# A four-layer network on one core: the first element's expert combination and first scan preparation spread over attention units, and the sorting's pool opened earlier

## The chip, the cores and the metric

The kernel runs on one core of a Trainium2 chip, in float32. The time is device microseconds (us) from start to end of one execution. A core has five engines that run beside each other, each with its own queue of instructions worked off in order: TensorE (PE, matrix products; its weight loads are listed as PEld), VectorE (DVE), ScalarE (ACT), GpSimd (POOL) and SyncE (SP, which issues most transfers). Engines wait for each other by semaphores. A waiting instruction holds everything behind it on its own engine. Matrix products go to a small accumulation memory (PSUM) of eight banks, which POOL does not read; all else lies in the on-chip memory SBUF, of 128 partitions.

## The reference

Four batch elements of 1024 tokens and 128 channels go through four layers. Each layer is a mixer and a feed-forward, each with a residual and a layernorm behind it:

```python
x = _layernorm(x + _L0_attn_ref(x, ...), axis=-1)   # two minGRU layers
x = _layernorm(x + _L0_ffn_ref(x, ...), axis=-1)    # routing to 64 slots
x = _layernorm(x + _L1_attn_ref(x, ...), axis=-1)   # attention of some queries
x = _layernorm(x + _L1_ffn_ref(x, ...), axis=-1)    # gated feed-forward
x = _layernorm(x + _L2_attn_ref(x, ...), axis=-1)   # 16-head linear attention
x = _layernorm(x + _L2_ffn_ref(x, ...), axis=-1)    # 8 experts, top 2 of them
x = _layernorm(x + _L3_attn_ref(x, ...), axis=-1)   # state-space scan
x = _layernorm(x + _L3_ffn_ref(x, ...), axis=-1)    # 8 experts, top-p of 0.8
```

The change touches the third layer's experts and the fourth layer's scan, whose cores are:

```python
# L2_ffn: two experts a token, weighted
y_sel = jnp.take_along_axis(y, indices[..., None], axis=2)
return (y_sel * weights[..., None]).sum(axis=2)
# L3_attn: x is RMS-normed; xc a causal convolution of x @ in_w.T over 4 tokens
xs = jax.nn.silu(xc.transpose(0, 2, 1))
delta = jax.nn.softplus(xs @ wd1.T @ wd2.T + wd2_b)
Bm = xs @ wb.T
Cm = xs @ wc.T
h = jnp.exp(d_l[:, :, None] * A) * h + (d_l * x_l)[:, :, None] * b_l[:, None, :]
y_l = jnp.einsum('ben,bn->be', h, c_l)
```

The scan has 256 channels and 16 states, so 16 x 256 recurrences over the tokens of each element.

## The kernel before, in words

**Attention of the third layer** (`l2_attn`, from L965). The work is 128 units: four elements, four quarters of 256 tokens each, eight pairs of heads. In iteration t of its loop the stages of neighbouring units are overlapped: `l2_project` of unit t+2 (PE product `pqk`; then the ACT relu of L1078 into `r_q` and `r_k`, and POOL's products `qt`, L1086), `l2_keys` and `l2_scores` of t+1 (`kN`, L1101; `pa_m`; DVE's mask `a`, L1144), `l2_before`, `l2_within` and `l2_out` of t (`po`, L1153; division on DVE). Every eight units `l2_values` makes the next quarter's values (`pv`, cast by DVE into `cv`), and every four `l2_project_out` transposes and projects the outputs (`pt`, `coT`, `pr`). The PE order of this part is the order in the program (a manual schedule). On the other engines, and in all that follows, a scheduler with a timeline model decides the order. `self.beat` is the latest unit's relu.

**Sorting** (`l2_dispatch`). After an element's attention its tokens are routed: softmax and ranks, positions by prefix sums, and 16 scatters on POOL (L1410, 128 rows of 512 bytes each) that put token rows into `xrows`, sorted by expert. For the first three elements each scatter has a dependency on the beat of its time, which spreads them; the last element's 16 are left in `self.m2["rest"]`, and the loop `l3` issues one per scan step. The dispatch's small tiles lie in the pool `md`, opened inside the attention's scope.

**Experts of the third layer** (`l2_ffn`, L1429). A generator works off 23 tiles of 128 sorted rows per element, advanced once per attention unit by `early(moe)`, and later per scan step. Per tile: two weight loads on SP (`wx`, L1485), row loads `xg` (L1469), transposes, the hidden products (into the attention's banks `pa_m`, later `ph`), ACT's sigmoid (L1517), the output products, store of results `ys` to `yrows` (L1539). It looks eight tiles ahead and waits there until the next element's rows are put. When an element's last tile is out, `l2_combine` (L1546) runs: 16 gathers on POOL (L1556) in two groups of 8 into the buffer `yg`, ACT copies scaled by the expert's weight (L1573, L1580), DVE additions of 128x512 (L1583, L1585), and the layernorm's parts (L163; square root on ACT at L177, normalisation at L187 and L191).

**Preparation of the scan** (`l3_prepare`, L1744). Once the first element is combined, the first of eight half-elements (element, half of 512 tokens) is prepared beside the last attention units, one generator step per unit: RMS norm, transposes `pt`, projection `pxe`, convolution of 3+1 terms on DVE, tanh, products `pdb` and `pd`, softplus by Exp and Ln on ACT (L1828, L1833), and DVE sums into `ud` and `dl`. `l3_early` tells where its tiles lie: in finished elements' transposed inputs `xT`, and in PSUM.

**Scan and fourth layer** (`l3`). For each half there are 16 steps, one per state (`l3_scan`, L1846): SP loads `bn` and `cn` (L1871, one row each spread over all partitions), POOL's product `db` (L1876, 128x1024), ACT's exponential `da` (L1880), two DVE scans (L1881), POOL's product `hc` (L1892), and PE's sum into `pys`. Beside the steps the loop advances the previous half's finish, the next half's preparation, the rest of the scatters, one expert tile (two in the first half) and the top-p experts of finished halves (`l3_experts`: weights `wh`, products `ph` and `py`, L2007, L2032). `l3` advances `moe` until an element is combined before it prepares that element's first half.

**Pools** (`program`, from L2194). Pools are opened and closed like a stack on either side of the memory: `keep`, `first`, `mt`, then `w2` (the attention's weights) on the right; `md` is opened inside `with w2`, and both are given back after the attention. `l3_pools` then opens the scan's pools over the room that has come free, so a scan tile waits for the last user of what lay there.

Of the kernel before, what the change touches and what calls it, by code (L numbers as in the profile page):

```python
# [12 lines left out]
F32 = mybir.dt.float32  # L13
# [3 lines left out]
ALU = mybir.AluOpType  # L17
# [3 lines left out]
P = 128  # L21
# [50 lines left out]
class Net:  # L72
# [874 lines left out]
    def l2_attn(self, load, dispatch, moe, first):  # L947
# [7 lines left out]
        with ExitStack() as ctx:  # L955
# [35 lines left out]
            for t in range(-2, n + 4):  # L991
                if t == 0:
                    load()
                if 0 <= t + 1 < n:
                    u = units[t + 1]
                    if u["hp"] == 0:
                        i = (t + 1) // NP2
                        if i + 1 < len(quarters):
                            nxt = quarters[i + 1]
                            self.l2_tiles(nxt, quarters[i])  # L1000
                            side.append(self.l2_values(nxt))
                    self.l2_keys(u)
                if 0 <= t + 2 < n:
                    self.l2_project(units[t + 2])
                if 0 <= t + 1 < n:
                    self.l2_scores(units[t + 1])
                if 0 <= t < n:
                    self.l2_before(units[t])
                    self.l2_within(units[t])
                if 0 <= t + 1 < n:  # L1010
                    self.l2_sums(units[t + 1])
                if "put" in self.m2["st"][0] if t > 0 else False:
                    early(moe)
                    if "done" in self.m2["st"][0]:
# [510 lines left out]
    def l2_expert_out(self, u, units, i, wp):  # L1525
# [12 lines left out]
        if j % 4 == n - 1:  # L1538
# [4 lines left out]
                in_=ys[:, 0:n, :],  # L1543
            )

    def l2_combine(self, st, wp):  # L1546

        nc, b = self.nc, st["b"]
        yg = {}

        def gather(h, c):
# [70 lines left out]
    def l3(self, moe, fp):  # L1622
# [98 lines left out]
    def l3_early(self, pool):  # L1721
# [5 lines left out]
        def at(name, shape):  # L1727
            if name in ("xnT", "tail", "xs3"):
                return pool.tile(shape, F32, name=name)
            if name in ("dl", "ud"):  # L1730
                return self.xT[1 if name == "dl" else 2].rearrange("p (e t) -> p e t", e=2)
            if name == "sq3":
# [3 lines left out]
            if name == "xc":  # L1736
                k[0] += 1
                return half(0, k[0] % 2)
            return half(0, name == "sp_w")[:, None, :]

        u = dict(b=0, h=0, at=at, ff=self.bank("pj"))
        self.c3["first"] = u
# [2 lines left out]
    def l3_prepare(self, u):  # L1745
# [2 lines left out]
        at, ff, dp = u.get("at", self.l3_at), u.get("ff", self.bank("ff")), c3["dp"]  # L1748
        wdb = c3["we"][:, :, 0:ND]

        sq = at("sq3", [P, 4, D])
        ms = self.sm.tile([P, 4], F32, name="ms3")
        for k in range(4):
            nc.scalar.activation(
                sq[:, k, :], self.xN[b][:, 4 * h + k, :], AF.Square, accum_out=ms[:, k : k + 1]
            )
        yield
        nc.scalar.activation(ms, ms, AF.Sqrt, bias=self.epsc, scale=1.0 / D)
        nc.vector.reciprocal(ms, ms)
        for k in range(4):  # L1760
            nc.scalar.activation(
                sq[:, k, :], self.xN[b][:, 4 * h + k, :], AF.Copy, scale=ms[:, k : k + 1]
            )
        yield
        pt = ff([P, 4, P], "pt")
        for k in range(4):
            self.tr(pt[:, k, :], sq[:, k, :])
# [2 lines left out]
            xnT, pt.rearrange("p a b -> p (a b)"), AF.Copy, scale=self.col("norm_w")  # L1770
        )
        yield

        K1 = KCONV - 1
        tail = at("tail", [P, 2, K1]) if h == 0 else u["prev"]["tail"]
# [2 lines left out]
        for ec in range(2):  # L1778
            p = ff([P, 512], "pxe")
            self.mm(p, c3["wskip"][:, 1, ec * P : (ec + 1) * P], xnT)  # L1780
            xc = at("xc", [P, 512])
# [4 lines left out]
            nc.vector.tensor_scalar(xc[:, o:], p[:, o:], w[K1], bias, ALU.mult, ALU.add)  # L1786
            if h:
                nc.vector.scalar_tensor_tensor(
                    xc[:, 0:K1], p[:, 0:K1], w[K1], tail[:, ec, :], ALU.mult, ALU.add
                )  # L1790
            for d in range(1, KCONV):
                nc.vector.scalar_tensor_tensor(
                    xc[:, d:], p[:, 0 : 512 - d], w[K1 - d], xc[:, d:], ALU.mult, ALU.add
                )
            if h == 0:
                nc.vector.tensor_scalar(
# [6 lines left out]
                    )  # L1803
            yield

            nc.scalar.activation(p, xc, AF.Tanh)
            nc.vector.scalar_tensor_tensor(xs[:, ec, :], p, 1.0, xc, ALU.add, ALU.mult)
# [9 lines left out]
        yield  # L1817

        dl, ud = at("dl", [P, 2, 512]), at("ud", [P, 2, 512])
        for g in ((0,), (1,)) if "at" in u else ((0, 1),):  # L1820
# [14 lines left out]
            for k, ec in enumerate(g):  # L1835
# [6 lines left out]
            if g[-1] == 0:  # L1842
                yield
        u.update(xnT=xnT, xs=xs, dl=dl, ud=ud, rows=rows)

    def l3_scan(self, u):  # L1846
# [351 lines left out]
def program(tc, io):  # L2198
    with ExitStack() as ctx:
# [9 lines left out]
        with ExitStack() as ff:  # L2209
# [37 lines left out]
```

## Time and profile before

| what | value |
|---|---|
| median of 3 runs | 2261.67 us (2253.73 to 2262.74) |
| the profiled execution | 2265.2 us, span 2263.4 us |
| mean granted PE clock | 0.934 |
| instructions | 46328 |
| attention units 105 to 109 begin, end | 1134.5, 1185.8 |
| last attention unit's projection begins | 1293.6 |
| first scan product `db` on POOL | 1363.5 |
| second half's first step | 1452.3 |
| first product of the top-p experts | 1525.1 |
| last scan product `hc` ends | 2126.8 |

The page's parts: totals per engine; the span in 40 slices; transfers; the chain of work that ended last; groups of instructions by source line with operands (`out<-in`, number, busy us, mean ns, idle time before them and its releaser). A line of the trace names engine, source line, operation and tile. Line numbers are those of the kernel shown. Sources are often helpers' lines, as L140 for every product and L177 for every square root of a layernorm, so the tile's name tells which one it is.

### The profile page before, as it was taken

The page shows a single profiled execution, that of the slowest core. Times are in us where ns is not written, and L with a number is a line of the kernel's source. Part 1 is how long each engine was busy: PE and PEld are TensorE (multiplying, and loading weights), DVE is VectorE, ACT ScalarE, POOL GpSimd, SP SyncE. Part 2 cuts the span into 40 slices and gives each one's busy share as a digit, 9 for nine tenths or more (in the row PEclk, how much of TensorE's full clock was granted, in tenths as well). Part 3 has the DMA queues.
Part 4 walks back from the last instruction along what each step waited for, and adds up shares of the span by engine and source line. Part 5 has one row for each costly group of instructions (what it writes and reads, how often), then busy time and mean ns, then how long its engine had stood idle before and what let it go on. Part 6 is the DMA issues. An engine that isn't in the chain of part 4 may idle for free.

```text
span 2263.4 us, 46328 instructions
## 1 busy us (share of the span) xinstructions
PE 1988.1 (88%) x17791; PEld 1392.3 (62%) x17791; DVE 1361.8 (60%) x3705; ACT 1184.6 (52%) x2578; POOL 1025.0 (45%) x813
## 2 busy tenths in 40 slices
PE   6778889899999999999979866688898999999998
PEld 3565555544577777787768654356565656565666
DVE  7767644433455654754555555696877688686522
ACT  6532434322344444454555556476768787676443
POOL 5100411000123244234143339989788889789400
PEclk9778979889999999999999987799999999999999
DMA  3010110050000000031222066466776676676421
GB/s 107 0 38 10 31 38 1 23 172 0 2 3 2 14 27 22 25 91 41 78 79 81 17 193 193 127 193 191 205 209 172 185 186 190 181 203 170 113 61 52
DMA packets 138605, 211.04 MB, mean 93 GB/s; under 512 B 18645, under 2 KB 75982, under 8 KB 137999
## 3 DMA queue, kind: packets, MB, share of 16 engines
q1 hardware_dynamic: 126238, 173.81, 25.4%
q0 software_dynamic: 12144, 34.26, 7.3%
q8 instruction: 140, 2.29, 0.4%
q14 instruction: 83, 0.67, 0.1%
HBM read 160.22 MB, written 23.16 MB: 81 GB/s over the span
## 4 chain that ended last, share of the span: by engine, by line
PE 44%; DVE 13%; ACT 10%; issue 3%; DMA 2%; POOL 1%; SPq 0%; DVEq 0%; ACTq 0%; POOLq 0%
PE py L140 8%; PE ph L140 7%; PE po L1153 5%; DVE db L1881 5%; PE pa_m L140 5%; PE pqk L140 5%; PE kp_mo L140 3%; PE pr L1223 2%; PE pys L140 2%; PE pv L140 2%; PE pt L144 1%; ACT da L1880 1%; ACT hh L2007 1%; PE kp_mo L144 1%; ACT xN L187 1%
## 5 line engine op out<-in xcount | busy, mean ns | idle before, releaser
L1086 POOL TENSOR_TENSOR qt<-r_q,sb_c_turn 128x256 f32<-128x256 f32 (+1 forms) x256 | 164.7, 664 | 451.0 <-ACT r_q L1078 447.1
L1892 POOL TENSOR_TENSOR hc<-db,cn 128x1024 f32<-128x1024 f32 x128 | 319.0, 2529 | 67.4 <-PE pys L140 26.8
L140 PEld LDWEIGHTS py<-wh,hh 128*128 128x128 f32 x2048 | 257.0, 196 | 79.8 <-issue 47.8
L1876 POOL TENSOR_TENSOR db<-ud,bn 128x1024 f32<-128x1024 f32 x112 | 293.1, 2679 | 7.6 <-ACT dl L1841 5.1
L140 PE MATMUL ph<-xT,wh 128*128 128x512 f32 x512 | 252.9, 611 | 24.0 <-ACT hh L2007 6.7
L140 PE MATMUL py<-wh,hh 128*128 128x128 f32 x2048 | 263.8, 280 | 10.8 <-ACT hh L2007 4.2
L2007 ACT ACTIVATE hh<-ph,sb_cols 128x512 f32<-128x512 f32 x256 | 170.3, 681 | 118.3 <-PE ph L140 92.1
L1144 DVE TENSOR_TENSOR a<-pa_m,sb_c_near 128x256 f32<-128x256 f32 x256 | 96.7, 419 | 201.4 <-PE pa_m L140 201.4
L1101 ACT ACTIVATE kN<-kp_mo,sb_c_trig 128x128 f32<-128x128 f32 x448 | 130.2, 372 | 130.6 <-PE kp_mo L144 122.4
L1880 ACT ACTIVATE da<-dl,aneg 128x512 f32<-128x512 f32 x224 | 153.6, 689 | 74.4 <-DVE db L1881 73.7
L140 PE MATMUL pys<-hc,sb_c_ident 128*128 128x512 f32 x324 | 160.6, 625 | 21.3 <-POOL hc L1892 17.9
L1881 DVE TENSOR_TENSOR_SCAN db<-da,carry,db 128x512 f32<-128x512 f32 x128 | 156.9, 1265 | 21.5 <-POOL db L1876 11.2
L1881 DVE TENSOR_TENSOR_SCAN db<-da,db 128x512 f32<-128x512 f32 x128 | 149.4, 1206 | 11.5 <-ACT da L1880 6.4
L140 PEld LDWEIGHTS ph<-xT,wh 128*128 128x128 f32 x512 | 88.0, 194 | 104.3 <-issue 49.0
L2032 DVE SCALAR_TENSOR_TENSOR h_acc<-py,gt,h_acc 128x128 f32<-128x128 f32 x252 | 70.8, 343 | 123.7 <-PE py L140 123.7
L140 PE MATMUL pqk<-xT,wE 128*128 128x256 f32 x512 | 136.4, 389 | 8.2 <-ACT coT L1220 4.2
L140 PEld LDWEIGHTS pys<-hc,sb_c_ident 128*128 128x128 f32 x324 | 61.1, 201 | 83.8 <-issue 57.7
L140 PEld LDWEIGHTS pqk<-xT,wE 128*128 128x128 f32 x512 | 88.5, 193 | 21.9 <-DVE cv L1063 8.1
L1220 ACT COPY coT<-pt 128x512 f32<-128x512 f32 x64 | 37.5, 587 | 116.8 <-PE pt L144 116.8
L140 PE MATMUL po<-ht,wD 128*128 128x512 f32 x192 | 92.9, 594 | 0.0
L1153 PE MATMUL po<-cv,a 128*64 128x65 f32 x2048 | 88.3, 228 | 0.0
L1556 POOL DMA_INDIRECT yg<-yrows,di x64 | 61.3, 957 | 57.5 <-DVE ch L1388 36.7
(463 smaller groups left out, 4255.2 us busy)
## 6 DMA issues: line engine op xcount, KB each, us to landing
wx<-in_wF SPq DMA_DIRECT2D x92, 384.0 KB, 3.4
bn<-rows SPq DMA_DIRECT2D x128, 256.0 KB, 4.7
cn<-rows SPq DMA_DIRECT2D x128, 256.0 KB, 4.2
wh<-in_wH SPq DMA_DIRECT2D x64, 512.0 KB, 3.8
hc<-hc POOLq DMA_DIRECT2D x47, 512.0 KB, 7.0
xrows<-zero SPq DMA_DIRECT2D x4, 1472.0 KB, 12.0
xg<-xrows SPq DMA_DIRECT2D x20, 256.0 KB, 3.6
yrows<-ys SPq DMA_DIRECT2D x20, 256.0 KB, 3.4
```

What stands on the lines that cost most here:

```text
L140: return self.nc.tensor.matmul(out=out, lhsT=lhsT, rhs=rhs, start=start, stop=stop)
L1086: nc.gpsimd.tensor_mul(u["qt"][:, m, a:], u["q"][:, a:], c2["turn"][:, m, o + a : o + 2 * P])
L1101: self.nc.scalar.activation(u["kN"][:, c, m, :], pk[:, c, :], AF.Copy, scale=trig[:, k, m : m + 1])
L1144: nc.vector.tensor_mul(u["a"][:, i, :, :], pa[i], self.c2["near"][:, None, :].to_broadcast([P, 2, P]),)
L1153: self.nc.tensor.matmul(out=u["po"][self.HALF[j], i, c, :], lhsT=lhsT, rhs=rhs, start=key not in u["begun"], stop=True, skip_group_check=True,
L1556: nc.gpsimd.indirect_dma_start(out=yg[h][:, k, c, :], out_offset=None, in_=st["out"][:, :], in_offset=bass.IndirectOffsetOnAxis(ap=st["des ...
L1876: nc.gpsimd.tensor_mul(db, ud, bc[0])
L1880: nc.scalar.activation(da, dl[:, ec, :], AF.Exp, scale=aneg[:, j : j + 1])
L1881: nc.vector.tensor_tensor_scan(db[:, ec, :], da, db[:, ec, :], carry[:, ec, n : n + 1] if h else 0.0, ALU.mult, ALU.add,)
L1892: nc.gpsimd.tensor_mul(hc, db, bc[1])
L2007: nc.scalar.activation(ht, ph, AF.Relu, bias=self.col("h_b1", i=e * NK + k))
L2032: nc.vector.scalar_tensor_tensor(acc[:, c, :], py[:, c, :], gt[:, c, e : e + 1], acc[:, c, :], ALU.mult, ALU.add,)
```

## The change

1. `l2_attn` advances the first preparation by a second step per unit.
2. `l2_ffn` is split: the tiles of elements 0 to 2, and behind their last combination those of element 3.
3. The first element's combination becomes a generator of its own, `l2_combine_first`. Its gathers, DVE multiply-adds (16 of 128x128 in place of 16 ACT copies and 4 DVE additions), one square root for all eight chunks, and four ACT and four DVE normalisations have a dependency on the beat of their unit. `yg0` (8 KB per partition) lies in `md`.
4. `l3` advances `rest`, the last element's scatters, only from the second half on.
5. The first preparation gets more steps and dependencies on the beat. The projection is copied from PSUM to SBUF by ACT, temporary tiles move into `md`, both channel halves share one Ln over 128x1024, and `dl` is summed in place instead of by a last ACT copy.
6. `md` is opened before the pool of the attention's weights.

```diff
@@ l2_attn
                     if next(g, self) is self:
                         side.remove(g)
+                if begin is not None:
+                    next(begin, None)
@@ l2_ffn
+        yield from self.l2_tiles_of(0, B - 1, wp)
+        yield from self.l2_tiles_of(B - 1, B, wp)
+
+    def l2_tiles_of(self, b0, b1, wp):
...
-            for st in self.m2["st"]
+            for st in self.m2["st"][b0:b1]
@@
+    def pace(self, i):
+
+        self.tc.add_manual_dep(i.ins, self.beat.name, SYNC, reason="spread out")
+        return i
+
+    def l2_combine_first(self, st):
...
+        def add(c):
+            for k in (1, 0):
+                self.pace(
+                    nc.vector.scalar_tensor_tensor(
+                        x[:, c, :], yg[:, k, c, :], st["wts"][k][:, c : c + 1], x[:, c, :],
+                        ALU.mult, ALU.add,
+                    )
+                )
+            v = self.sm.tile([P, 4, 6], F32, name="ln_st")
+            nc.vector.bn_stats(v[:, 0, :], x[:, c, :])
+            nc.vector.bn_aggr(mv[:, c, :], v[:, 0, :])
+
+        for c in range(NC + 3):
+            for k in range(2 if c < NC else 0):
+                self.pace(
+                    nc.gpsimd.indirect_dma_start(
...
+            if c >= 3:
+                add(c - 3)
+            yield
+        yield
+        self.pace(nc.scalar.activation(rs, mv[:, :, 1], AF.Sqrt, bias=self.epsc))
+        yield
+        yield
+        self.pace(nc.vector.reciprocal(rs, rs))
+        nc.vector.scalar_tensor_tensor(nm, mv[:, :, 0], -1.0, rs, ALU.mult, ALU.mult)
+        yield
+        yield
+        for c in range(0, NC, 2):
+            self.pace(
+                nc.scalar.activation(
+                    x[:, c, :], x[:, c, :], AF.Identity, bias=nm[:, c : c + 1], scale=rs[:, c : c + 1]
+                )
+            )
+            self.pace(
+                nc.vector.tensor_scalar(
+                    x[:, c + 1, :], x[:, c + 1, :], mv[:, c + 1, 0:1], rs[:, c + 1 : c + 2],
+                    ALU.subtract, ALU.mult,
+                )
+            )
+            yield
+        st["done"] = True
@@ l3
-                        next(moe)
+                        next(moe, None)
...
-                for k in range(1):
+                if i:
                     next(self.m2["rest"], None)
@@ l3_early
+            if name in ("sp_u", "sp_w", "tmp"):
+                return self.m2["md"].tile(shape, F32, name=f"e_{name}")
@@ l3_prepare
+            if early:
+                t = at("tmp", [P, 512])
+                nc.scalar.copy(t, p)
+                p = t
+                yield
...
+        if early:
+            yield
+            us, v = at("sp_u", [P, 2, 512]), at("sp_w", [P, 2, 512])
+            t = at("tmp", [P, 2, 512])
...
+            pace(nc.scalar.activation(v, v, AF.Ln))
+            for ec in range(2):
+                yield
+                d = dl[:, ec, :]
+                pace(nc.vector.tensor_sub(t[:, ec, :], us[:, ec, :], t[:, ec, :]))
+                pace(nc.vector.tensor_add(d, d, t[:, ec, :]))
+                pace(nc.vector.tensor_add(d, v[:, ec, :], d))
+                pace(nc.vector.tensor_mul(ud[:, ec, :], xs[:, ec, :], d))
@@ program
             w2 = ExitStack()
+            md = w2.enter_context(tc.tile_pool(name="moed", bufs=1, side="right"))
             n.l2_attn_load(w2.enter_context(tc.tile_pool(name="w2", bufs=1, side="right")))
...
         with w2:
-            md = w2.enter_context(tc.tile_pool(name="moed", bufs=1, side="right"))
             n.l2_attn(load, n.l2_dispatch, moe, first)
```

More of the change, by code (lines that the diff above doesn't have):

```diff
@@ L1544, in l2_expert_out @@
             )
+    def pace(self, i):
+        self.tc.add_manual_dep(i.ins, self.beat.name, SYNC, reason="spread out")
+        return i
+    def l2_combine_first(self, st):
+        nc, b, md = self.nc, st["b"], self.m2["md"]
+        yg = md.tile([P, 2, NC, D], F32, name="yg0")
+        mv = md.tile([P, NC, 2], F32, name="mv0")
+        rs = md.tile([P, NC], F32, name="rs0")
+        nm = md.tile([P, NC], F32, name="nm0")
+        x = self.xN[b]
+        def add(c):
[13 more added lines that the diff above has]
+                    nc.gpsimd.indirect_dma_start(
+                        out=yg[:, k, c, :],
+                        out_offset=None,
+                        in_=st["out"][:, :],
+                        in_offset=bass.IndirectOffsetOnAxis(
+                            ap=st["dest"][k][:, c : c + 1], axis=0
+                        ),
+                    )
[21 more added lines that the diff above has]
+                    ALU.subtract, ALU.mult,
+                )
+            )
+            yield
+        st["done"] = True
@@ L1546, in l2_combine @@
     def l2_combine(self, st, wp):
         nc, b = self.nc, st["b"]
+        if b == 0:
+            yield from self.l2_combine_first(st)
+            return
         yg = {}
@@ L1738, in at @@
                 return half(0, k[0] % 2)
-            return half(0, name == "sp_w")[:, None, :]
         u = dict(b=0, h=0, at=at, ff=self.bank("pj"))
@@ L1749, in l3_prepare @@
         wdb = c3["we"][:, :, 0:ND]
+        early = "at" in u
+        pace = self.pace if early else (lambda i: i)
         sq = at("sq3", [P, 4, D])
@@ L1753, in l3_prepare @@
         for k in range(4):
-            nc.scalar.activation(
-                sq[:, k, :], self.xN[b][:, 4 * h + k, :], AF.Square, accum_out=ms[:, k : k + 1]
+            pace(
+                nc.scalar.activation(
+                    sq[:, k, :], self.xN[b][:, 4 * h + k, :], AF.Square, accum_out=ms[:, k : k + 1]
+                )
+            )
+            if early and k == 1:
+                yield
+        yield
+        pace(nc.scalar.activation(ms, ms, AF.Sqrt, bias=self.epsc, scale=1.0 / D))
+        if early:
+            yield
+        pace(nc.vector.reciprocal(ms, ms))
+        for k in range(4):
+            if early and k % 2 == 0:
+                yield
+            pace(
+                nc.scalar.activation(
+                    sq[:, k, :], self.xN[b][:, 4 * h + k, :], AF.Copy, scale=ms[:, k : k + 1]
+                )
             )
         yield
[L1758 to L1764, printed above, removed]
+        if early:
+            yield
         pt = ff([P, 4, P], "pt")
@@ L1772, in l3_prepare @@
         yield
+        if early:
+            yield
         K1 = KCONV - 1
@@ L1780, in l3_prepare @@
             self.mm(p, c3["wskip"][:, 1, ec * P : (ec + 1) * P], xnT)
+            if early:
+                t = at("tmp", [P, 512])
+                nc.scalar.copy(t, p)
+                p = t
+                yield
             xc = at("xc", [P, 512])
@@ L1785, in l3_prepare @@
             o = K1 if h else 0
-            nc.vector.tensor_scalar(xc[:, o:], p[:, o:], w[K1], bias, ALU.mult, ALU.add)
+            pace(nc.vector.tensor_scalar(xc[:, o:], p[:, o:], w[K1], bias, ALU.mult, ALU.add))
             if h:
@@ L1791, in l3_prepare @@
             for d in range(1, KCONV):
-                nc.vector.scalar_tensor_tensor(
-                    xc[:, d:], p[:, 0 : 512 - d], w[K1 - d], xc[:, d:], ALU.mult, ALU.add
+                if early and d == 2:
+                    yield
+                pace(
+                    nc.vector.scalar_tensor_tensor(
+                        xc[:, d:], p[:, 0 : 512 - d], w[K1 - d], xc[:, d:], ALU.mult, ALU.add
+                    )
                 )
@@ L1804, in l3_prepare @@
             yield
-            nc.scalar.activation(p, xc, AF.Tanh)
-            nc.vector.scalar_tensor_tensor(xs[:, ec, :], p, 1.0, xc, ALU.add, ALU.mult)
+            pace(nc.scalar.activation(p, xc, AF.Tanh))
+            if early:
+                yield
+            pace(nc.vector.scalar_tensor_tensor(xs[:, ec, :], p, 1.0, xc, ALU.add, ALU.mult))
+            yield
+        if early:
             yield
@@ L1819, in l3_prepare @@
         dl, ud = at("dl", [P, 2, 512]), at("ud", [P, 2, 512])
-        for g in ((0,), (1,)) if "at" in u else ((0, 1),):
+        if early:
+            yield
+            us, v = at("sp_u", [P, 2, 512]), at("sp_w", [P, 2, 512])
+            t = at("tmp", [P, 2, 512])
+            for ec in range(2):
+                p = ff([P, 512], f"pd{ec}")
+                self.mm(p, c3["wd2"][:, ec * P : (ec + 1) * P], db[0 : DDELTA + 1, :])
+                nc.scalar.activation(us[:, ec, :], p, AF.Abs)
+                nc.vector.tensor_single_scalar(dl[:, ec, :], p, 0.0, ALU.max)
+                yield
+                pace(nc.scalar.activation(us[:, ec, :], us[:, ec, :], AF.Exp, scale=-1.0))
+                pace(
+                    nc.scalar.activation(
+                        v[:, ec, :], us[:, ec, :], AF.Identity, bias=self.ones[:, 0:1]
+                    )
+                )
+                yield
+            for ec in range(2):
+                pace(
+                    nc.scalar.activation(t[:, ec, :], v[:, ec, :], AF.Identity, bias=c3["neg1"])
+                )
+            yield
+            pace(nc.scalar.activation(v, v, AF.Ln))
+            for ec in range(2):
+                yield
+                d = dl[:, ec, :]
[3 more added lines that the diff above has]
+                pace(nc.vector.tensor_mul(ud[:, ec, :], xs[:, ec, :], d))
+        for g in () if early else ((0, 1),):
             us, v = at("sp_u", [P, len(g), 512]), at("sp_w", [P, len(g), 512])
@@ L1841, in l3_prepare @@
                 nc.scalar.copy(dl[:, ec, :], p)
-            if g[-1] == 0:
-                yield
         u.update(xnT=xnT, xs=xs, dl=dl, ud=ud, rows=rows)
```

## The prediction

> **What bounds the kernel now.** The profiled execution took 2265.2 us (span 2263.4); the median of the three runs shown is 2261.67, 3.5 lower, and every sum below is made against 2265.2 and then lowered by 3.5. I read the page's totals first, to see which engine is nearest to the span; then busy time by stretch, cut at the stages; then the chain, the waits and POOL's instructions only where the change works.
>
> ```profile
> PE 1988.1 (88%) x17791; PEld 1392.3 (62%) x17791; DVE 1361.8 (60%) x3705; ACT 1184.6 (52%) x2578; POOL 1025.0 (45%) x813
> ```
>
> TensorE (PE) is the bound on average, but POOL's 45% is an average over stages. The stretches (us; then busy time of PE, weight loads, DVE, ACT, POOL with instruction counts, then granted clock, DMA share, GB/s):
>
> ```profile
> 941.00:974.60 33.60, 32.17 (x521) 26.68 (x520) 24.41 (x104) 15.71 (x50) 7.21 (x12) 1.00 0.25 70
> 1134.50:1185.80 51.30, 37.30 (x520) 29.85 (x519) 29.18 (x130) 30.12 (x89) 22.47 (x28) 0.90 0.29 80
> ...
> 1238.40:1301.60 63.20, 52.32 (x929) 41.53 (x932) 34.09 (x99) 34.82 (x77) 22.07 (x28) 0.92 0.08 23
> 1301.60:1363.50 61.90, 37.22 (x336) 33.59 (x326) 32.31 (x128) 31.06 (x79) 22.11 (x23) 0.83 0.67 208
> 1363.50:1441.00 77.50, 52.64 (x178) 30.01 (x178) 52.95 (x78) 49.02 (x106) 71.32 (x38) 0.81 0.53 158
> 1441.00:1525.10 84.10, 65.83 (x265) 41.15 (x265) 68.76 (x114) 50.94 (x101) 77.74 (x36) 0.86 0.54 164
> 1525.10:2126.80 601.70, 551.46 (x2722) 362.17 (x2721) 451.23 (x868) 434.89 (x785) 526.11 (x273) 0.97 0.69 188
> 2126.80:2263.40 136.60, 124.30 (x691) 88.64 (x689) 34.51 (x124) 57.23 (x94) 0.00 (x0) 0.98 0.19 56
> ```
>
> Row 1 is attention units 73 to 77, row 2 is units 105 to 109: the same five places one element later, with the same matmuls (521 and 520). In row 2 the first element's combination runs beside them, and they take 17.7 us longer. Row 3 is units 118 to 127, the last ten, beside the first preparation: 10.9 us of PE idle, clock 0.92. Rows 4 to 6 lead from the end of the attention over the first three scan stretches to the first top expert's matmul at 1525.1: PE is idle 24.7, 24.9 and 18.3 us, and from 1363.5 on POOL is busy 92%, so there **POOL** is the bound. From 1525.1 PE is busy 92% and 91%: PE is the bound to the end.
>
> What stalls row 2 stands in the chain (start, us, what):
>
> ```profile
> 1146.36 4.07 DMA yg<-yrows,di
> 1150.76 0.39 ACT yg L1580
> 1151.17 0.69 DVE yg L1583
> ...
> 1172.45 2.55 DMA yg<-yrows,di
> ...
> 1180.13 1.28 ACT L177
> ```
>
> ACT and DVE are queues in order. An ACT copy that waits for a gather's landing holds the next unit's relu and feature copies behind it, and PE waits for those.
>
> Of rows 4 and 5, POOL's instructions in order of time and two waits (engine, line, releaser: total, times, longest):
>
> ```profile
> 1342.27 0.95 POOL L1556 DMA_INDIRECT yg<-yrows,di  x1 [0.30 <-issue]
> 1343.52 0.94 POOL L1556 DMA_INDIRECT yg<-yrows,di  x1 [0.30 <-issue]
> 1344.77 0.99 POOL L1410 DMA_INDIRECT xrows<-xN,di  x1 [0.30 <-DVE wt L1404]
> ...
> 1362.54 0.96 POOL L1410 DMA_INDIRECT xrows<-xN,di  x1 [0.30 <-issue]
> 1363.52 2.37 POOL L1876 TENSOR_TENSOR db<-xT,bn 128x1024 f32<-128x1024 f32 x1
> ```
> ```profile
> POOL yg L1556 <- DVE ch L1388: 36.7, 1, 36.7
> ```
> ```profile
> SPq L1871 <- DVE wt L1404: 6.0, 1, 6.0
> PE ph L140 <- DMA wx<-in_wF: 13.2, 3, 11.9
> ```
>
> One gather or scatter costs POOL 1.26 us from start to start. POOL stands idle 36.7 us, then issues 8 gathers and 15 scatters before the first scan product `db` at 1363.52. That product also waits for `bn`, whose load SP could not issue before 1344.82, when the last dispatch's `wt` was done: the scan's tiles lie where the dispatch's pool lay.
>
> **Part 1, combination paced.** It removes 16 ACT copies (0.41 us), 4 DVE adds (0.70 us), and one of two square roots; it adds 16 DVE multiply-adds of 128x128, an estimated 0.34 us each by the h_acc row (343 ns), 5.5 us in all, in places set by the relu. The 16 gathers stay, but 16 in two bursts become 8, 4 and 4 behind single units. Of the 17.7 us, one table-load pair stays (unit 116 holds such a pair and takes 8.06 us where unit 76 took 5.80: 2.3), and the preparation's pair, which stood in these units, now stands in unit 115 (2.3). Gathers land 2.4 to 4.1 us after issue and DVE's multiply-adds follow within a unit of some 6 us, so I leave 3 us of stalls. Gain 17.7 - 4.6 - 3 = **10**. Ends: 17.7 if all is hidden; -3 if waiting multiply-adds hold DVE's cast `cv` and its mask `a`, which the next unit's matmuls need, four times as in the 3.25 and 4.92 us waits of DVE at 1151 and 1161.
>
> The row says a table load is 1.28 us, and its pair lengthens a unit by 2.3. The Trainium skill ("ScalarE: Activation LUTs", What ACT_TABLE_LOAD costs) speaks against part 1 being worth that much: it counts about 1.38 us of drain beside every load, 2.66 a switch, so by estimate two pairs would take 10.6 instead of 4.6 and the gain would be 4. I go by the row: PE has matmuls queued meanwhile.
>
> **Part 2, preparation paced.** One Ln over 128x1024 (an estimated 1.1 us by doubling the 0.63 row) replaces two Exp/Ln rounds; of four loads at 1278.66, 1289.64, 1294.10 and 1298.17 two stay, at the end of unit 127. Two steps a unit spread it over units 112 to 127. Two ACT copies out of PSUM are added (1.2 us), two into `dl` taken away (1.2 us). Gain **8** of the 10.9 us idle; ends 2 and 14 (all idle, and the clock from 0.92 to 1.00, some 4 us, less the 1.1). The added waits are on ACT's relu: on ACT itself nothing is queued in a new order, on DVE the unit's own mask stands behind, which waits for the same relu's product anyway.
>
> **Part 3, pool ahead.** Count from T = 1293.6, the last unit's projection. The changed SP order has the `bn` load right behind the `xg` load that ran at 1316.3, waiting only for the last element's normalisation (done 1318.6). So `bn` goes at T+25, lands some 6 us later, and the first `db` is at T+31 instead of T+69.9: 39 us earlier. But POOL now has the 16 gathers of the second element and 14 scatters inside the first half's scan, 30 x 1.26 = 37.8 us where 2 scatters (2.5) stood. Scan products are 32 x 2.36 = 75.5. Before, half 1 began at 1452.3, T+158.7. Now: 31 + (75.5 + 37.8)/0.94 = T+152; 0.92 to 0.96 of POOL gives T+149 to T+154. The experts' first matmul is behind the first half's finish, so it comes **7** earlier than T alone says. Half 1 has 16 gathers instead of 8: +10, so half 2 starts where it did. Ends: 39 earlier, if all thirty issues fit beside; 40 later, if POOL waits (see the rivals).
>
> The trace does not show `db` beside the dispatch's DVE work. Its rows give 2.35 us for `db` from 1363 to 1525 (DVE 68 to 82% busy), and 2.68 over all 112; at 2.68 and `hc`'s 2.53 half 0 would take 8 us more, all of the 7. The Trainium skill ("GPSIMD Engine Reference", Specifications) says that POOL shares its SBUF interface with VectorE and that DVE instructions with two SBUF inputs contend; it points to this loss, without a price. I take 2.36, since in these stretches DVE's load is alike.
>
> **Part 4, last scatters and tiles.** The put-off by `if i:` is in the program text, but the scheduled POOL order keeps all 14 inside half 0; it costs nothing and gives nothing. Splitting the tile list makes the last element's 23 tiles start only behind the third's combination. Before, 2 of them ran ahead of 1525.1; now none: 2 x 2 us (a unit with a tile is 5.5 to 5.8, without 3.9) = **4** us more PE work in the PE-bound part. Nothing covers that.
>
> **Sum.** 10 + 8 + 7 - 4 = 21, and 1 for the clock (0.81 to 0.86 in rows 5 and 6) where PE is less idle: 2265.2 - 22 = 2243, on the median 2240.
>
> **Rivals.**
> 1. *POOL waits inside half 0* (slower). The scatters wait for the dispatch on DVE, whose order now has five steps of scans (12.3 us) ahead of `wt`; POOL is in order, so `db` and `hc` stand behind. For: in row 2, POOL's share fell to 44% when gathers and `qt` were mixed. Against: in the order, the first scatter comes after some 10 products and 8 gathers, at T+31+34 = T+65, and `wt` was done at T+51, with the 12.3 T+63. Price: half 0 at a share s takes 113.3/s; at 0.70 half 1 starts at T+193, 34 late: -18 + 34 + 4 = +20, 2282 on the median. It makes the kernel slower by 0.5% (11 us) from s = 0.74 down: 31 + 113.3/0.74 = T+184, 25 late.
> 2. *The head start passes through.* For: PE idles 68 us in rows 4 to 6, and the 11.9 us wait for `wx` lies behind the blocked SP. Against: POOL at 92%. If POOL's issues overlap with waits, FFN starts 30 early: -18 - 30 + 4 = -44, 2218.
> 3. *Most is given back* (same). The combination gains 4 (landing waits moved from ACT to DVE), the preparation 5, the transition 0 because of the 8 us of slower products, tiles -4: -5, 2257. For: PE is bound at 92% after 1525 and takes no gain there.
> 4. *The pool move frees nothing*: `bn` is still late, since SP is in order and the `wx` loads ahead of it wait for PE (18.3 us for one of them in these 70 us). If it went at T+51 as now, the first `db` would be at T+57 with the thirty issues still inside: half 1 at 57 + 120.5 = T+178, 19 late, -18 + 19 + 4 = +5, 2267. Against: the `xg` load just ahead ran at 1316.3.
>
> **How the numbers follow.** About 0.5% (11 us) is what a measurement of this kernel can tell from no change: faster is below 2250, slower above 2273. Forecast 2240 (own range 2230 to 2250): 0.48. Rival 2: 0.13. Rival 3: 0.16, of which 0.05 is below 2250. Rival 4: 0.08. Rival 1: 0.15. Faster: 0.48 + 0.13 + 0.05 = 0.66. Same: 0.11 + 0.08 = 0.19. Slower: 0.15. The range reaches from 2212 (below it only the far half of rival 2) to 2270 (above it rival 1).
>
> **What would show it.** Units 105 to 109 near 41 us instead of 51.3; the last ten units near 55; first `db` at T+31; POOL busy over 90% until half 1 begins at T+152; first expert matmul at T+224; PE 91 to 92% busy behind it. Wrong: DVE idle for `yg` landings over 2 us a time; POOL idle in half 0 for `wt` or for a scan; experts' start later than T+240.

## The result: 1.1% slower, and the loss stands behind the fourth half

The changed kernel takes 2286.01 us (median of 4 runs, 2284.64 to 2287.07) against 2262.2 for the kernel before in the same comparison: 1.0107 of it, with an interval of 1.0087 to 1.0126. Its profiled execution has a span of 2285.3 us. The page's totals, to be held against those of before:

```profile
PE 1998.1 (87%) x17791; PEld 1394.7 (61%) x17791; DVE 1377.3 (60%) x3715; ACT 1176.5 (51%) x2556; POOL 1028.4 (45%) x813
```

The work is nearly the same: as many matmuls and POOL instructions, ten DVE instructions more and 22 ACT instructions less. So the loss must lie in where the work stands. These are the same stretches as in the prediction, at the changed kernel's own marks (us; busy PE, weight loads, DVE, ACT, POOL with counts; clock, DMA share, GB/s):

```profile
1135.80:1182.00 46.20, 35.36 (x521) 28.85 (x520) 32.37 (x133) 15.87 (x50) 22.67 (x28) 0.93 0.32 89
1182.00:1237.40 55.40, 50.84 (x858) 42.93 (x858) 31.08 (x109) 37.87 (x106) 19.47 (x26) 1.00 0.30 84
1237.40:1293.30 55.90, 48.91 (x889) 38.83 (x887) 31.72 (x91) 30.34 (x71) 24.13 (x28) 0.97 0.08 24
1293.30:1318.60 25.30, 21.16 (x250) 19.40 (x251) 13.36 (x51) 13.88 (x40) 0.03 (x1) 0.93 0.50 141
1318.60:1439.50 120.90, 79.57 (x319) 54.86 (x318) 86.31 (x165) 67.28 (x154) 101.81 (x63) 0.79 0.61 184
1439.50:1521.30 81.80, 52.53 (x178) 27.48 (x177) 58.19 (x109) 49.46 (x101) 71.20 (x42) 0.83 0.51 148
1521.30:2144.20 622.90, 563.12 (x2756) 367.52 (x2756) 457.13 (x857) 433.28 (x775) 524.67 (x265) 0.96 0.67 182
2144.20:2285.30 141.10, 128.79 (x717) 91.95 (x715) 38.01 (x139) 59.56 (x96) 0.86 (x2) 0.98 0.22 62
```

Units 105 to 109 went from 51.3 to 46.2, the last ten from 63.2 to 55.9. The first scan product came 45 us earlier. And yet the top-p experts start only 3.8 us earlier (1521.3), and from there to the end it takes 764.0 us instead of 738.3. Of the 18 us that parts 1 and 2 of the prediction promised ahead of T, the last attention unit's projection, 8.3 came; the experts' start, counted from T, is 4.4 later where part 3 had it 7 earlier; and the 25.7 behind it stand where part 4 had 4 and the clock was to give 1 back.

The sharpest cut is at the start of the fifth half (called half 4, as halves are counted from 0), where the scan of the third element begins. Before, then after, from T on:

```profile
1293.60:1756.00 462.40, 368.99 (x1937) 248.23 (x1938) 327.58 (x665) 307.86 (x627) 373.08 (x209) 0.90 0.63 182
1756.00:2263.40 507.40, 470.46 (x2371) 314.14 (x2369) 316.89 (x659) 321.60 (x548) 325.62 (x161) 0.97 0.55 149
```
```profile
1285.30:1747.90 462.60, 364.97 (x1856) 241.60 (x1856) 335.55 (x646) 294.99 (x592) 360.26 (x195) 0.89 0.62 177
1747.90:2285.30 537.40, 485.97 (x2453) 324.45 (x2451) 322.16 (x682) 336.38 (x585) 339.74 (x175) 0.97 0.54 146
```

From T to half 4 both take 462.5 us, and the changed kernel does 81 matmuls and 14 POOL instructions less in them (first counts: PE 1937 against 1856; last counts: POOL 209 against 195). It does them behind half 4, which takes 30.0 us more: PE is busy 15.5 longer and idle 14.5 longer. The account: T is 8.3 earlier, T to half 4 is 0.2 longer, half 4 to the end 30.0 longer, together +21.9, which is the difference of the spans.

What lies behind half 4 now and did not before:

```profile
L140 PE MATMUL ph<-xgT,wx x48: 273/275/313, 1749.1 to 1785.6; 128*128 128x128 f32 x48
```
```profile
L1628 POOL DMA_INDIRECT yg<-yrows,di x16: 943/947/1092, 1803.5 to 1852.9; - x16
```
```profile
1747.90:2285.30 537.40, 11.19 (x80) 10.54 (x80) 0.97 0.54 146
```

The first line is 48 hidden products of 8 to a tile: six expert tiles of the last element. The second is all 16 gathers of its combination. The third is PE's time behind half 4 with every product of the tile weights `wx`: 11.19 us. In the kernel before, `wx` is used by no PE instruction behind half 4.

### The profile page after: what moved, and what is told of

Its sections match the earlier page's. It is cut to its first block, busy times and chain, and to the rows that moved or that the text cites. A ratio compares the mean times of both kernels' runs of the same rounds, so it can differ in the third digit from the quotient of the medians.

```text
span 2285.3 us, 46312 instructions
## 1 busy us (share of the span) xinstructions
PE 1998.1 (87%) x17791; PEld 1394.7 (61%) x17791; DVE 1377.3 (60%) x3715; ACT 1176.5 (51%) x2556; POOL 1028.4 (45%) x813
## 3 DMA queue, kind: packets, MB, share of 16 engines
q8 instruction: 140, 2.29, 0.4%
## 4 chain that ended last, share of the span: by engine, by line
PE 42%; DVE 16%; ACT 9%; issue 3%; POOL 2%; DMA 1%; SPq 0%; DVEq 0%; ACTq 0%; POOLq 0%
PE py L140 7%; PE ph L140 7%; DVE db L2011 5%; PE po L1155 5%; PE pqk L140 5%; PE pa_m L140 4%; PE kp_mo L140 3%; PE pv L140 2%; PE pr L1225 2%; PE pys L140 2%; PE pt L144 1%; ACT da L2010 1%; PE kp_mo L144 1%; ACT hh L2137 1%; DVE h_acc L2162 1%
## 5 line engine op out<-in xcount | busy, mean ns | idle before, releaser
L2006 POOL TENSOR_TENSOR db<-ud,bn 128x1024 f32<-128x1024 f32 x112 | 285.8, 2599 | 40.2 <-DVE ud L1972 29.3
L140 PE MATMUL ph<-xT,wh 128*128 128x512 f32 x512 | 258.8, 623 | 17.2 <-ACT hh L2137 4.9
L140 PE MATMUL pys<-hc,sb_c_ident 128*128 128x512 f32 x324 | 166.2, 641 | 22.6 <-POOL hc L2022 16.0
L140 PE MATMUL pa_m<-r_q,r_k 64*64 64x128 f32 x2048 | 86.8, 285 | 1.6 <-DVE mh L1526 1.6
```

What stands on the lines that cost most here:

```text
L140: return self.nc.tensor.matmul(out=out, lhsT=lhsT, rhs=rhs, start=start, stop=stop)
L2006: nc.gpsimd.tensor_mul(db, ud, bc[0])
```

## Experiments

Kernels of one group ran on one chip beside the kernel before, whose median stands with the group; ratios are to it. The groups fell on different chips, so ratios are compared, and times only inside a group. A ratio and its interval are taken over the group's runs, so a ratio can differ by up to 0.2% from that of the medians. The expectations speak of three theories: A, the division of the tile list costs the time; B, POOL's thirty gathers and scatters inside the first half cost it; C, every edit makes the planner order the scan's instructions anew, and the orders differ in time.

### Which part costs the time (before: 2260.14)

**e1**, the tile list undivided and the scatters not put off:
```diff
-        yield from self.l2_tiles_of(0, B - 1, wp)
-        yield from self.l2_tiles_of(B - 1, B, wp)
+        yield from self.l2_tiles_of(0, B, wp)
...
-                if i:
-                    next(self.m2["rest"], None)
+                next(self.m2["rest"], None)
```


> The changed kernel with the tile list undivided again and the last element's scatters advanced from the first half on; the paced combination and preparation and the earlier pool stay. Theory A (the division of the tile list costs the time: 9 tiles leave the first two scan stretches of the second half, where PE idles 25 us, and run behind the start of the top-p experts, where PE is the bound): about 26 us come back, 2255 to 2262, and PE idle in the first stretch of the second half falls from 25 to under 12 us. Theory B (POOL's thirty gathers and scatters inside the first half delay the scan and through it the experts): nothing comes back, 2280 to 2288.

Measured 2262.84, 1.0009 (0.9996 to 1.0023). PE idle in the first stretch of the second half: 8.7 us of 40.5, against 25.5 of 63.0. Without these two edits the kernel cannot be told from the one before; it lies 0.8 us above theory A's range. Which of the two it is, e5 and e9 ask.

**e2**, the pool in its old place, all else as changed (the `md` line moved back into `with w2`).


> The changed kernel with the sorting's pool opened where it was before; all else as changed. Theory A: still slow, since the tile list is still divided: 2275 to 2290. Theory B: the gathers and scatters go ahead of the first scan product again, so the loss goes and the attention's 8 us remain: 2252 to 2262.

Measured 2281.49, 1.0095 (1.0079 to 1.0112): theory A. **e3**, the kernel before with only the pool moved ahead:


> The kernel before with only the pool opened earlier. Theory A: no loss, the scan starts some 40 us earlier and gives most of it back: 2250 to 2263. Theory B: the whole loss behind the attention, 2275 to 2290.

Measured 2261.69, 1.0006 (0.9996 to 1.0016). The first scan product comes at T+29.7 instead of T+69.9, the second half at T+148.4 instead of T+158.7, the top-p experts at T+230.9 instead of T+231.5, and nothing of it reaches the end. Theory B falls, and the hope of part 3 in this kernel with it.

**e4**, only the paced parts (e1 and e2 together).


> Only the paced combination and preparation remain of the change: pool in its old place, tile list undivided, scatters as before. Both theories: the attention's gain alone, about 8 us, 2252 to 2256. If it is above 2262, the gain of the attention is lost in the scan for a third reason (another order of the same work).

Measured 2269.29, 1.0034 (1.0014 to 1.0054). The attention ends 8.5 us earlier, as expected, and the kernel is slower all the same: neither theory had this. e1 differs from e4 by the pool alone and lies lower (1.0009 against 1.0034), but the two intervals overlap, so that a gain of the pool is there neither shown nor excluded.

### One part at a time (before: 2262.31)

**e5**, only the division:
```diff
+        yield from self.l2_tiles_of(0, B - 1, wp)
+        yield from self.l2_tiles_of(B - 1, B, wp)
+
+    def l2_tiles_of(self, b0, b1, wp):
...
-            for st in self.m2["st"]
+            for st in self.m2["st"][b0:b1]
```


> The kernel before with only the tile list divided (elements 0 to 2, then 3). Theory A (division costs the time): no gain of the attention and the whole loss of some 23 us, 2276 to 2290, PE idle above 13 us in the second half's first stretch, no expert tile between the second half's start and the start of the top-p experts. If the loss needs the other parts too, 2258 to 2270.

Measured 2278.56, 1.0063 (1.0046 to 1.0080): the division loses by itself, less than in the whole change. Its other signs came too: PE idles 14.9 us in the second half's first stretch, and no expert tile runs between the second half's start and the top-p experts.

**e6**, only the preparation (e4 without the call of `l2_combine_first`), **e7**, only the combination (e4 with `l3_early`, `l3_prepare` and the single step of before), **e8**, e7 with the pool ahead.


> The kernel before with only the paced preparation, two steps a unit. Theory C (the planner orders the scan's instructions anew for every change ahead of it, and the order it found for the paced preparation stalls 10 us more): the program order of the scan is here the one of the run with both paced parts, so the attention ends 3 to 5 us earlier and the total is still higher, 2266 to 2275. Rival (the added loss of that run came from the combination's tiles): 2255 to 2260.

> The kernel before with only the paced first combination. Theory C: attention 5 us shorter, scan order near the one of before (105 of 2000 PE rows differ against 325 with the paced preparation), so the gain passes through: 2253 to 2259. Rival (every gain ahead of the scan is lost in it): 2259 to 2264.

> The paced first combination and the pool opened earlier, preparation and tile list as before. If both gains add (5 us of the attention, nothing for the pool): 2253 to 2259. By theory C the order of the scan is again another one (467 of 2051 PE rows differ), so that it can lie anywhere from 2250 to 2272, with the difference to the attention's gain standing behind the start of the top-p experts.

Measured: e6 2276.64, 1.0066 (1.0046 to 1.0086); e7 2275.24, 1.0044 (1.0026 to 1.0062); e8 2268.6, 1.0030 (1.0020 to 1.0040). e6 has the sign that theory C gave it and not its rival's, but lies 1.6 us above the range, and its attention ends 9.1 us earlier (T = 1284.5) instead of 3 to 5. e7 missed: its combination is 7.5 us shorter (units 105 to 109 take 43.8), but the unpaced preparation gives that back in the units behind (T is 161.3 us behind unit 105, before 159.1), and the part behind T is 8.1 us longer although few rows of the order moved. How many rows move tells nothing of the price. e8 missed the sum of the gains and lies in theory C's wide range; against e7 (1.0044) the pool's move makes no difference that is clear of the intervals.

### Division or putting off, and the order by itself (before: 2294.43, a slower chip)

**e9**, the list undivided, but `if i:` kept.


> The changed kernel with the tile list undivided, but the last element's scatters still advanced only from the second half on. The tiles of the third and fourth element then wait in the generator for the last scatter to be issued in the program, so the order has again no expert tile in the second half. Theory A (what costs is expert tiles missing where PE idles, not the division as such): 69 to 70 tiles before the top-p experts begin, 2272 to 2288. If only the division counts (late last combination, its 16 gathers in one stretch): 2258 to 2266, as without both.

Measured 2290.01, 0.9981 (0.9966 to 0.9996). Only 61 tiles run ahead of the top-p experts here, fewer than in the changed kernel (69), and it costs nothing: the experts start early, at T+212.6, and all 92 tiles are done by half 4, though its 16 last gathers stand behind half 4 as in the changed kernel. The rival's forecast holds ("only the division counts"), and theory A's wording falls: tiles missing before the experts' start do not foretell the time. What fits instead is the tiles left at half 4; that this is the reason is read from the traces below.

**e10**, the kernel before with one exchange in `l3`; **e11** and **e12**, the same exchange in e4 and e1:
```diff
-                next(moe, None)
-                if i == 0:
-                    for k in range(1):
-                        next(moe, None)
                 for k in range(4 if n % 8 == 7 else 3):
                     next(work)
+                next(moe, None)
+                if i == 0:
+                    for k in range(1):
+                        next(moe, None)
```


> The kernel before with one change that leaves all work and everything ahead of the scan as it is: in each scan step the top-p experts are advanced ahead of the expert tile and not behind it, so the planner finds another order of the same instructions. Theory C (orders of the same work differ by some 10 us, and the order of before is a good one): up to the first scan product as before, 2266 to 2280. Rival (the end is set by the work, not by its order): 2258 to 2266.

> The same exchange in the kernel that has only the two paced parts (2269 before the exchange). Theory C: another order again, and it can be a better one: anywhere from 2252 to 2280, with the attention ending as there, so that the difference stands wholly behind the start of the top-p experts. Rival: within 3 us of 2269.

> The same exchange in the changed kernel with undivided tile list and early scatters (2263 before the exchange). Theory C: anywhere from 2248 to 2275; below 2255 it would beat both kernels. Rival: within 3 us of 2263.

Measured: e10 2298.51, 1.0020 (1.0003 to 1.0038); e11 2297.71, 1.0018 (1.0003 to 1.0032); e12 2276.08, 0.9927 (0.9904 to 0.9949). The expected times were for the usual chip, so only the ratios can be read. e11 (1.0018) was on another chip than e4 (1.0034), too near to tell whether the exchange did anything there.

### The same side by side (before: 2299.62, another slower chip)

> The changed kernel again, beside the next three on one chip. 1.0107 of the kernel before in the first measurement: 1.008 to 1.013 expected. On a chip where it is within 0.5% of the kernel before, the loss depends on the chip and not on the order of the tiles alone.

> Undivided tile list and early scatters again (1.0009 of the kernel before when measured first): 0.998 to 1.003, so that the division's price stays about 1%.

> The same with the exchanged order (0.9927 of the kernel before on the slow chip). Theory C (order worth about 10 us): again 0.990 to 0.997, some 12 us below the one without exchange. If the ratio was the chip's: 0.998 to 1.004, like the one without exchange.

> The kernel before with the exchanged order (1.002 on the slow chip). Theory C: its own order as good or bad as chance has it, 0.997 to 1.008; up to the first scan product as before.

Measured: the changed kernel 2309.25, 1.0047 (1.0029 to 1.0064); e1's kernel 2294.23, 0.9979 (0.9965 to 0.9994); e12's 2284.67, 0.9941 (0.9922 to 0.9961); e10's 2304.85, 1.0032 (1.0016 to 1.0048). The division, with the scatters put off, costs 15 us here. The changed kernel missed its range (1.008 to 1.013) and lies within 0.5% of the kernel before, so by that expectation's own rule the size of the loss depends on the chip too. e1's kernel lies just below its range (0.998 to 1.003), e12's and e10's in theirs. The order alone, same work and same front, is worth 9.6 us (f2 to f3) in one kernel and 5 us the other way in another (f4).

### Is it an unlucky order of the divided list? (before: 2261.24)

> The changed kernel with the exchanged order in each scan step and the list still divided. Theory A (position of the tiles): the order again has no expert tile in the second half, so the time stays 0.5 to 1.3% above the next kernel's, and above the kernel before or within 0.5% of it. If the changed kernel only met an unlucky order: within 0.3% of the next kernel.

> Undivided list, early scatters, exchanged order, for the third time (0.9927 and 0.9941 of the kernel before, on chips where that takes 2294 and 2300). 0.990 to 0.997 again where the kernel before takes over 2290; on a chip where it takes 2262, 0.995 to 1.002.

Measured: divided in the exchanged order 2299.91, 1.0189 (1.0167 to 1.0211); undivided in the exchanged order 2257.74, 0.9990 (0.9976 to 1.0004). With the division (and the scatters put off) it is 42 us slower than without, so it loses in both orders, and by more than the 0.5 to 1.3% expected. The rival, an unlucky order of the changed kernel alone, falls. The divided kernel's two lines from T to half 4 and from there:

```profile
1278.00:1751.00 473.00, 370.24 (x1883) 246.46 (x1882) 339.43 (x649) 296.95 (x596) 359.94 (x194) 0.90 0.61 174
1751.00:2291.10 540.10, 483.98 (x2430) 324.59 (x2428) 322.87 (x681) 330.49 (x580) 339.78 (x175) 0.95 0.54 144
```

and e1's, undivided:

```profile
1286.20:1748.90 462.70, 369.66 (x1938) 249.03 (x1937) 341.77 (x670) 307.52 (x628) 374.32 (x209) 0.91 0.63 182
1748.90:2265.10 516.20, 472.25 (x2371) 315.19 (x2369) 317.12 (x659) 321.85 (x551) 325.54 (x161) 0.97 0.54 147
```

POOL's count behind half 4 shows the 16 gathers, 175 with the division and 161 without. Over all kernels, from the traces (T is the start of the last projection, half 4 that of its first `db`; the windows above begin up to 0.5 us ahead of these):

| kernel | tiles done by half 4 (of 92) | gathers left | T to half 4 | half 4 to end | PE idle in it |
|---|---|---|---|---|---|
| before | 92 | 0 | 462.4 | 507.4 | 36.9 |
| after; f1 | 86; 86 | 16; 16 | 462.5; 462.7 | 537.4; 537.3 | 51.4; 52.1 |
| g1 | 86.8 | 16 | 473.1 | 539.5 | 56.1 |
| e2, old pool | 86 | 16 | 454.5 | 537.6 | 49.3 |
| e5, division alone | 88 | 16 | 460.7 | 523.4 | 48.7 |
| e9, put off alone | 92 | 16 | 472.3 | 517.8 | 46.0 |
| e1; f2 | 92; 92 | 0; 0 | 462.8; 471.5 | 516.0; 515.0 | 44.0; 44.5 |
| e12; f3; g2 | 92 | 0 | 464.5; 465.5; 464.1 | 510.2; 509.1; 510.8 | 41.4; 41.9; 42.5 |
| e3, pool alone; e8 | 92 | 0 | 456.0; 457.5 | 510.8; 510.3 | 42.9; 40.4 |
| e4; e6; e7 | 92 | 0 | 466.3; 467.5; 461.3 | 516.1; 522.7; 516.6 | 47.0; 46.3; 47.2 |
| e10; f4; e11 | 92 | 0 | 484.0; 484.2; 480.6 | 509.5; 509.0; 512.9 | 40.5; 43.2; 44.6 |

The runs with some 86 tiles need 537 to 540 us behind half 4, those with all tiles and gathers done 507 to 523. In pairs that differ by the division and the put-off alone it is 21.4 us (after, e1), 22.3 (f1, f2) and 28.7 (g1, g2). That f1 and f2 lie only 15 us apart in the end comes from ahead of half 4, where f2 takes 8.8 us longer than f1. e5, with four tiles left, needs hardly longer behind half 4 (523.4) than e6 with none (522.7), so there the tiles left at half 4 are not shown to be the reason.

## Why the prediction was wrong, step by step

**Part 4, the term that failed.** I took 2 tiles at 2 us behind the experts' start, 4 us. It was 4 tiles behind that start (69 done instead of 73). The price of a tile was about right: from there on, products with `wx` keep PE busy for 39.06 us instead of 33.21, and transposes of `xg` for 3.49 instead of 2.29, together 7.1 us, 1.8 a tile. But I stopped counting there. I had the order in which the last element's tiles start only behind the third combination, but looked at how many lie behind the experts' start, not at when the last one is done. Six tiles and the last combination's 16 gathers moved over half 4, and from there the kernel takes 30.0 us longer. Of the 15.5 us that PE is busy longer there, the six tiles are 11.7 (products 11.19, transposes 0.49). The other 14.5 us are idle time, at which I had put nothing.

Against e1, which has all but the division and the put-off, 21.4 us behind half 4 are 13.7 of busy PE and 7.4 of idle PE. The gathers stand in the eighth to the sixteenth step of half 4, here in the changed kernel and then the same steps in e1:

```profile
1786.50:1863.90 77.40, 70.37 (x346) 46.57 (x345) 48.44 (x107) 52.73 (x108) 60.53 (x41) 0.96 0.66 171
```
```profile
1792.40:1852.60 60.20, 49.11 (x206) 31.54 (x207) 46.68 (x88) 48.09 (x92) 43.91 (x23) 0.91 0.64 176
```

They take 17.2 us longer (before: 49.7 us in all), but hold 140 matmuls more, and PE idles less in them (7.0 against 11.1 us); the steps ahead of them are 4.9 us shorter. So it is PE's work that fills them, not a wait for the gathers. The remaining 8.9 us come later, and 8.2 of them are idle PE. One thing goes with the late combination in every trace: behind half 4 POOL idles 24.5 to 54.6 us ahead of its `db` products, mostly until DVE's `ud`, in the kernels with the 16 gathers left (40.2 in the changed one), and 6.1 to 11.6 in all others. That this wait is what keeps PE idle is not shown; e9 has it too (27.5) and no loss.

The division with the put-off costs 15 us (f1 against f2), some 22 (the ratios of the changed kernel and e1, from two chips) or 42 (g1 against g2).

**Part 3, the scan's start** was right to half 1 and wrong behind it. The first product came at T+33 (T+31), once `bn` landed; half 1 began at T+154 (T+152):

```profile
1318.57 6.94 POOL L2006 TENSOR_TENSOR db<-xT,bn 128x1024 f32<-128x1024 f32 x3 [29.62 <-DMA bn<-rows]
...
1361.28 2.37 POOL L2022 TENSOR_TENSOR hc<-db,cn 128x1024 f32<-128x1024 f32 x1
1363.82 1.01 POOL L1412 DMA_INDIRECT xrows<-xN,di  x1 [0.17 <-issue]
1365.13 0.99 POOL L1412 DMA_INDIRECT xrows<-xN,di  x1 [0.30 <-issue]
1366.14 2.36 POOL L2006 TENSOR_TENSOR db<-xT,bn 128x1024 f32<-128x1024 f32 x1
```

Scatters stand between the products, and POOL's pause ahead of each is 0.3 us at most. The issues (32 here, 16 gathers and 16 scatters) took most of the head start, as worked out. I had misread how many stood in the first half before: not 2 scatters, but 8 gathers and 1 scatter; the sum does not use this number. But I let the experts start a fixed time behind the first half. They are advanced with the scan's steps, and begin behind 24 to 29 `hc` products in every kernel here; so they begin in the second half, and there the first eight steps held 16 gathers where before they held none: 63.0 us instead of 37.7, with PE idle for 25.5 of them.

```profile
1439.50:1502.50 63.00, 37.53 (x141) 21.00 (x140) 44.95 (x84) 32.58 (x66) 52.40 (x34) 0.82 0.54 158
```

They began at T+236, not T+224. e3 shows the same of the pool alone: its head start of 40 us is 10 at the second half's start, 0.6 at the experts' and none at the end (1.0006).

**Part 1** gave 5.1 us where 10 stood, and 2.8 of them went in the next eight units (52.6 to 55.4), which hold six table loads instead of two: the combination's pair and the preparation's, which I had priced at 4.6, and the attention's own. The stalls were larger than the 3 us I left: units 107 to 109 are 5.1 us shorter, but 105 and 106 together as long as before (23.2 us). The chain through units 105 and 106:

```profile
1141.42 3.38 DMA yg<-yrows,di
1144.96 0.15 issue
1145.17 0.70 DVE cv L1065
1145.91 1.15 PE pqk L140 x4
...
1149.26 2.31 DVE xN L1568 x2
...
1152.77 0.21 DVE st L1127
1153.01 0.30 DVE st L1130
1153.35 1.22 PE kp_mo L140 x4
```

A gather took 3.38 us to land; DVE stood idle for the last 1.84 of them with the cast `cv` behind the waiting multiply-add, and its multiply-adds then kept the state's sums `st` from PE, which waited 3.08 us for them. The wait moved from ACT to DVE, the mechanism of the range's lower end, at a smaller price than there.

**Part 2** was right: 7.3 us for 8, and 6.1 of them are idle time of PE up to T (10.9 before, 4.8 now). The clock in the rows of the last ten units rose from 0.92 to 0.97.

**Rivals.** Rival 1 had the right sign and size (2282) by the wrong mechanism: in half 0 POOL was busy for 101.8 of 120.9 us, paused 8.3 between issues and waited 10.5 in four waits ahead of `hc`, none for `wt`; by the rival's own count s is 113.3/120.9 = 0.94, where it needed 0.74. Its "for" was misread too: POOL's share in row 2, 44%, is higher than in row 1 (21%). Rivals 2 and 4 did not come: `bn` was early, and the head start was given back. Rival 3 was right in one point, that PE's bound takes no gain from ahead of it: of the 8.5 us that e4 gains before T, none reaches the end. Of the signs of being wrong, DVE's longest wait for a landing in units 105 to 109 was 1.84 us and the experts came at T+236, both short of the marks; only POOL's wait for a scan in half 0 (4.1 us) showed. No sign stood where the loss came, behind half 4. The POOL rate (2.35 us a `db` in half 0) stayed as in the quiet rows, so the loss that the Trainium skill ("GPSIMD Engine Reference", Specifications) points to did not show beside the dispatch. Its price for a table switch ("ScalarE: Activation LUTs", What ACT_TABLE_LOAD costs) would by estimate make four more loads 10.6 us; the eight units with them are 2.8 longer, and unit 110, which holds one of these pairs, takes 6.27 us in both kernels.

**What stays open.** How the loss behind half 4 is shared between tiles and gathers was not run apart: the division without the put-off was measured only in the kernel before (e5), and no run left tiles without gathers. Kernels with all tiles and gathers done do the same work behind half 4 in 507 to 523 us. That the order found by the planner makes such differences is shown at 9.6 us (f2 against f3) and 5 (f4 against the kernel before on that chip). That it is the cause in e4, e6 and e7 is argued from this: the source of that part is unchanged and the tiles are all done, but no run held the order fixed. Why e5 loses some 14 to 16 us and the whole change 24, with the same division, is not told apart either. On the two slower chips e10, f4 and e11 take 480 to 484 us from T to half 4, more than any other kernel; no trace of the kernel before was taken there, so f4's 5 us cannot be placed.

The version without division and with the exchanged order (e12) is faster than the kernel before on two chips (0.9927 and 0.9941), and than the changed kernel on the one of them where that ran too (f1); on a third it cannot be told from no change (0.9990, 0.9976 to 1.0004).

## What to carry to other kernels

Where work is spread as filler over later stages, ask of every delayed piece when its last one is done, not how many lie behind the next mark: here the 11.7 us of PE work in six tiles passed over into a stage where PE was busy over 90%, and the 81 matmuls fewer ahead of it shortened nothing there. A stage's start that is advanced with another stage's steps moves with those steps and not with its data. And a head start is worth what the engine behind it has free: POOL had 32 issues to place among the first half's products, and the 40 us of e3 bought nothing.

## What the runs showed of the hardware

The kernel before takes 2260 to 2262 us on three of the chips and 2294 and 2300 on two others. In e1's kernel, the same program on two chips, the last projection starts at 1286.4 and 1304.7, and units 105 to 109, with the gathers, take 43.9 and 53.6; from T to half 4 it is 462.8 and 471.5, and from half 4 on there is no slowing (516.0 and 515.0). Ratios from different chips differ by up to 0.6% (the changed kernel 1.0107 and 1.0047), more than their intervals.
